# VectorE's side work dealt out slot by slot, and one head of a search copied by ScalarE

## The chip, the cores and the metric

One core of one Trainium2 chip runs the whole program. The metric is device microseconds of one execution, as the median over several runs. TensorE (PE, with its weight loads PEld), VectorE (DVE), ScalarE (ACT), GpSimd (POOL) and SyncE (SP, which only issues DMAs here) run side by side and wait for each other by semaphores.

## The reference

One transformer block with modulation from a condition `c`, in fp32: 4 sequences of 2048 tokens, 256 channels, 8 heads of 32; then a mixture of experts with 2 shared and 16 routed experts of width 128, 4 of them for each token.

```
mod = (silu(c) @ wmod) -> sa, ca, ga, sb, cb, gb
ga, gb = sign * max(|.|, 0.25)
h = layernorm(x) * (1 + ca) + sa
x = x + ga * attn(h)        # causal softmax(q k / sqrt(32) + head_scale * geo(q, k)) @ v, then @ w_out
h = layernorm(x) * (1 + cb) + sb
x = x + gb * ffn(h)
ffn(h): shared = sum over 2 experts of gelu(h @ up) @ down
        probs = softmax(h @ router); gate = the 4 largest probs, else 0
        routed = sum over 16 experts of (gelu(h @ up) * gate) @ down
```

## The kernel before

**Tiling.** The tokens are 16 blocks of 512 rows (`QB`), four to a sequence; block i has place qb = i mod 4 in its sequence and sees qb + 1 blocks of keys. The 8 heads are two groups (g = 0, 1) of four, whose 32 rows each lie in the four row groups of TensorE.

**Searches.** Softmax needs each row's maximum first. `max_steps` makes one search step for 128 queries, 512 keys and four heads: `scores(t, ch)` computes the scores into two PSUM places (`ps`, each of two heads, 128x1024), and VectorE adds the causal mask where the step lies on the diagonal and reduces each place to its maxima (`parts`). When a group's steps are done, `split` and `turn` carry the maxima to TensorE as three bf16 pieces (`mT`). Block i + 1's steps run while block i is worked on.

**Sums.** `sum_steps(i, g, oT)` has one slot for each 128 keys: `probabilities(kb)` multiplies scores of four heads into two PSUM places (`st`), takes the maxima off in the same accumulation, and ScalarE's exps write `p`; `weigh(kb, 0)` and `weigh(kb, 1)` add to the numerators (`av`) and denominators (`dv`). After a group's last slot `finish` (line 735) copies both out of PSUM (ScalarE `num`, VectorE `rd`), and VectorE takes one reciprocal and one product of 128x512 into `oT`. A block has ks = 8, 16, 24 or 32 slots, half of them for each group.

**PSUM.** Three places of two banks go round (`pair`, tag m) for `ps`, `st` and small products during the sums; two single banks (`accp`) hold `av` and `dv`, and in the stretches between the sums every small product (`single`).

**Order.** It is written out by hand, and every engine keeps its program order (`Pinned`). For each block there are two stretches:

- *Between the sums* (`fill_in`): projections of a coming block, the router's logits and the shared experts of block i - 2, tiles of the routed experts, the output product of block i - 1, and as many search steps as that work covers.
- *The sums*: `part` is a list of (place, step), sorted by place. Slot n's scores stand at n, its weighted sums at n + 1.3 and n + 1.6, the searches that are left (`rest`) at n + 0.5, and ticks at n + 0.9. The side work of VectorE is strung along by `when`, from assumed durations: the first norm of coming blocks, the router's choice for block i - 2 (`choice_steps`), at a group's end its places (`place_steps`), and the second norm of block i - 1.

**Experts.** Routed tokens are handled in five groups of 2, 3, 3, 3 and 3 blocks; the last two blocks go through all experts densely. For a group `place_steps` finds each token's row in a buffer sorted by expert, and GpSimd scatters the rows there, 16 indirect DMAs and one load for each block (`scatters`). When the last is issued `tiles_of` starts the group's expert tiles (`px`, `pu`, `py`), whose rows and weights SyncE fetches. The results are gathered by GpSimd and added up by VectorE (`combine`, result `sum`). `tick` issues one scatter or gather, and lets a combine run two ticks after its last gather.

**Names in the profile.** The recording helper gives all lines as L52 (L72 for the scatters), so groups are told apart by tile names: `pk` and `pc` are the products that count tokens of an expert, `selb` and `seen` their inputs, `rank` the copy of `pk`; `xnb` the second norm's rows, `ptb` their transposes; `rsb` the norm's power.

Of the kernel before, what the change touches and what calls it, by code (L numbers as in the profile page):

```python
# [19 lines left out]
P = 128  # L20
# [72 lines left out]
def adaln_block_kernel(  # L93
# [324 lines left out]
    def max_steps(i, g):  # L418
# [6 lines left out]
        def scores(t, ch):  # L425
# [15 lines left out]
            for a, both in enumerate(halves):  # L441
                if ch == qb:
                    edge = both[:, :, w - P : w]
                    nc.vector.tensor_tensor(edge, edge, c_pair, ALU.add)
                nc.vector.tensor_reduce(
                    parts[:, t, 2 * a : 2 * a + 2, ch], both[:, :, :w], AX.X, ALU.max
                )
# [51 lines left out]
    def tick(add=True):  # L499
        for due in sums_due:  # L500
            due[0] -= 1
        if add and sums_due and sums_due[0][0] <= 0:
            sums_due.pop(0)[1]()
        if scatters:
            scatters.pop(0)()
            return
        if not gathers and ready and len(sums_due) < 2:
            gathers.extend(ready[0][0])
        if gathers:
            gathers.pop(0)()  # L510
            if not gathers:
                sums_due.append([2, ready.pop(0)[1]])
# [150 lines left out]
    def sum_steps(i, g, oT):  # L663
# [5 lines left out]
        pts = {}  # L669
# [46 lines left out]
        def weigh(kb, s):  # L716
# [15 lines left out]
            if s and kb == nkb - 1:  # L732
                finish()

        def finish():
            rd = once.tile([P, QB], F32, tag="rd", name=f"rd{i}_{g}")
            num = once.tile([P, QB], F32, tag="num", name=f"num{i}_{g}")
            nc.scalar.copy(num, sums[0])
            nc.vector.tensor_copy(rd, sums[1])
            nc.vector.reciprocal(rd, rd)  # L740
            nc.vector.tensor_tensor(oT[:, g, :], num, rd, ALU.mult)

        return [
# [6 lines left out]
        ]  # L750

# [68 lines left out]
    def turn_steps(i):  # L820
# [14 lines left out]
        def logits():  # L835
# [10 lines left out]
            logs[i] = small.tile([P, TT, R], F32, tag="log", name=f"log{i}")  # L846
# [4 lines left out]
    def choice_steps(i, group):  # L851
# [18 lines left out]
        def choose():  # L870
# [7 lines left out]
            top = small.tile([P, TT, 8], F32, bufs=1, tag="rtop", name=f"rtop{i}")  # L878
            rest = small.tile([P, TT, R + 8 - TOPK], F32, bufs=1, tag="rrest", name=f"rrest{i}")
            for t in range(TT):  # L880
                nc.vector.max(top[:, t, :], pr[:, t, :])
                nc.vector.match_replace(rest[:, t, :], top[:, t, :], pr[:, t, :], -1.0)
            sel = small.tile([P, TT, R], F32, bufs=1, tag="sel", name=f"sel{i}")
            nc.vector.tensor_scalar(sel, rest[:, :, :R], 0.0, None, ALU.is_lt)
# [11 lines left out]

        def count():

            sel = held["sel"]
# [4 lines left out]
        def earlier_ones():  # L904
            selb = held["selb"]
            t0 = group.blocks.index(i) * TT
# [8 lines left out]
            nc.vector.tensor_copy(group.rank[:, t0 : t0 + TT], pk)  # L915
            for t in range(TT):
                nc.vector.tensor_tensor(group.seen, group.seen, selb[:, t, :], ALU.add)

        def weights():

            pr, sel = held["pr"], held["sel"]
            t0 = group.blocks.index(i) * TT
            met = small.tile([P, TT, R], F32, bufs=1, tag="met", name=f"met{i}")
            flat = sel.rearrange("p t e -> p (t e)")
# [3 lines left out]
            hot = group.hot[:, t0 : t0 + TT]  # L928
            shape = [P, TT, TOPK, R]
            nc.vector.tensor_tensor(  # L930
                hot,
# [4 lines left out]
            nc.vector.tensor_tensor(hot, hot, sel.unsqueeze(2).broadcast_to(shape), ALU.mult)  # L936
            wide = once.tile(shape, F32, tag="hotp", name=f"hotp{i}")
            nc.vector.tensor_tensor(
                wide, hot, pr[:, :, :R].unsqueeze(2).broadcast_to(shape), ALU.mult
# [17 lines left out]
        steps = [differences, exponentials, choose]  # L957
        if group is not None:
            return steps + [count, weights, earlier_ones]
        return steps + [across]  # L960

    def place_steps(group):

        n, tok = group.n, group.tok
        held = {}

        def tiles_of_experts():
            pc = single([P, R], f"pc{n}")
            nc.tensor.matmul(pc, lhsT=unit3, rhs=group.seen, start=True, stop=True)
            ci = small.tile([P, R], I32, bufs=1, tag="ci", name=f"ci{n}")  # L970
            nc.vector.tensor_scalar(ci, pc, float(P - 1), None, ALU.add)
# [10 lines left out]
        def owners():  # L982
            shape = [P, MAXT, R]
            past = once.tile(shape, BF16, tag="num", name=f"past{n}")
            nc.vector.tensor_tensor(
                past,
                tile_no.unsqueeze(2).broadcast_to(shape),
# [3 lines left out]
            who = small.tile([P, MAXT], F32, bufs=1, tag="who", name=f"who{n}")  # L991
            nc.vector.tensor_reduce(who, past, AX.X, ALU.add)
            nc.vector.tensor_scalar(group.owner, who, float(R - 1), None, ALU.min)

        def places():
            shape = [P, tok, R]
            rank, hot = group.rank[:, :tok], group.hot[:, :tok]
            nc.vector.tensor_tensor(
                rank, rank, held["first"].unsqueeze(1).broadcast_to(shape), ALU.add
            )  # L1000
            shape = [P, tok, TOPK, R]
            nc.vector.tensor_tensor(hot, hot, rank.unsqueeze(2).broadcast_to(shape), ALU.mult)
            at = small.tile([P, 3 * TT, TOPK], F32, bufs=1, tag="atf", name=f"atf{n}")
# [538 lines left out]
```

## Time and profile before

| what | us |
|---|---|
| median of 5 runs (2571.86 to 2588.51) | 2586.14 |
| the profiled execution | 2581.32 |
| its span, first to last instruction | 2579.6 |
| the sixteen sums together | 1262.1 |
| the stretches between, before and after | 1317.5 |
| of these, from the last sums to the end | 273.2 |
| mean granted TensorE clock | 0.95 |

The costliest groups of VectorE and ScalarE in the profiled execution:

| group | count | mean ns | busy us |
|---|---|---|---|
| VectorE maxima, 128x1024 | 448 | 1221 | 530.1 |
| VectorE maxima, narrower | 192 | 426 to 959 | 133.0 |
| VectorE mask on the diagonal, 128x256 | 256 | 427 | 109.3 |
| VectorE reciprocal of the denominators, 128x512 | 32 | 3353 | 107.3 |
| ScalarE exps, 128x1024 | 448 | 1021 | 434.2 |

How to read it: the span is one execution on the chip. An engine's busy time is a mean over stretches with different limits, so the share of VectorE (55%) does not say where it is late. The granted clock tells in which time TensorE ran at half speed. A wait is put down to what came last.

### The profile page before, as it was taken

To read this page: it belongs to the slowest core of one execution; us is meant where nothing else is said; L and a number is where in the kernel's file an instruction comes from. 1 tells how busy PE (TensorE), PEld (TensorE's weight loads), DVE (VectorE), ACT (ScalarE), POOL (GpSimd) and SP (SyncE) were. 2 spreads that over 40 slices of the span, in tenths; PEclk is the share of its full clock that TensorE was granted. 3 is DMA by queue.
4 is the path that set the end of the run, shared out by engine and by line. 5 is a ranking of instruction groups with operands and counts; after the bars stand their busy time and mean duration, and the time that the engine had idled before them with its cause. 6 is when DMAs were issued, how large, how long until landed. Compare 5 with 4: busy or idle time off the path is not lost.

```text
span 2579.6 us, 42345 instructions
## 1 busy us (share of the span) xinstructions
PE 2412.5 (94%) x16961; PEld 1171.5 (45%) x16961; DVE 1406.6 (55%) x2609; ACT 978.7 (38%) x1372; POOL 702.0 (27%) x740
## 2 busy tenths in 40 slices
PE   7999999999999899999999999999898999998987
PEld 4433423345544223355654335254544643335754
DVE  5576655526676845247564666346664564422235
ACT  2223233543343234544343334543343345453320
POOL 3201010411133134202014422401442025544324
PEclk9889899999999899999999999998999999998999
DMA  2300401434432112223641225233636843236943
GB/s 86 117 1 9 147 9 59 139 123 147 157 120 64 39 54 81 74 74 102 228 133 66 82 96 180 74 104 99 206 128 210 260 146 95 89 135 234 329 151 110
DMA packets 219701, 306.90 MB, mean 119 GB/s; under 512 B 18544, under 2 KB 158832, under 8 KB 219504
## 3 DMA queue, kind: packets, MB, share of 16 engines
q1 hardware_dynamic: 192720, 228.89, 26.8%
q0 software_dynamic: 25536, 73.43, 8.9%
q8 instruction: 134, 2.20, 0.3%
q10 hardware_dynamic: 1248, 1.86, 0.2%
q14 instruction: 63, 0.52, 0.1%
HBM read 193.49 MB, written 114.82 MB: 120 GB/s over the span
## 4 chain that ended last, share of the span: by engine, by line
PE 77%; DVE 10%; ACT 4%; issue 4%; POOL 2%; DMA 2%; another core or an unknown queue 0%; SPq 0%; POOLq 0%; ACTq 0%; DVEq 0%
PE st L52 15%; PE ps L52 12%; PE av L52 10%; PE dv L52 8%; PE pu L52 7%; PE py L52 5%; DVE parts L52 4%; PE po L52 3%; PE ppq L52 2%; PE px L52 2%; PE pv L52 2%; PE ppk L52 2%; PE pd_s L52 1%; PE pd L52 1%; ACT p L52 1%
## 5 line engine op out<-in xcount | busy, mean ns | idle before, releaser
L52 DVE TENSOR_REDUCE parts<-ps 128x2 f32<-128x1024 f32 (+3 forms) x640 | 662.6, 1062 | 357.9 <-PE ps L52 336.4
L52 ACT ACTIVATE p<-st 128x1024 f32<-128x1024 f32 (+3 forms) x640 | 538.8, 893 | 677.9 <-PE st L52 628.8
L52 PE MATMUL st<-qT,kv 32*128 32x512 f32 (+3 forms) x2560 | 428.4, 597 | 33.5 <-DVE parts L52 18.6
L52 PE MATMUL ps<-kv,qT 32*128 32x512 f32 (+3 forms) x2560 | 390.5, 610 | 19.3 <-DVE parts L52 10.1
L52 POOL DMA_INDIRECT got<-yg,at x224 | 220.1, 983 | 396.0 <-ACT p L52 128.2
L52 PE MATMUL av<-p,kv 128*32 128x512 f32 (+3 forms) x2560 | 318.7, 566 | 6.7 <-issue 3.0
L52 PE MATMUL dv<-p,ones 128*32 128x512 f32 (+3 forms) x2560 | 311.5, 553 | 1.3 <-issue 1.1
L72 POOL DMA_INDIRECT xg<-rows,at x219 | 213.2, 973 | 292.5 <-ACT p L52 133.6
L52 PEld LDWEIGHTS st<-qT,kv 32*128 32x128 f32 x2560 | 143.9, 191 | 302.9 <-issue 211.1
L52 DVE TENSOR_TENSOR ps<-ps,cmask 128x256 f32<-128x256 f32 x256 | 109.3, 427 | 264.0 <-PE ps L52 234.6
L52 PEld LDWEIGHTS ps<-kv,qT 32*128 32x128 f32 x2560 | 128.6, 192 | 211.6 <-issue 110.6
L52 POOL TENSOR_TENSOR x<-x,tmps 128x512 f32<-128x512 f32 x28 | 35.4, 1263 | 621.4 <-DVE tmps L52 621.4
L52 PE MATMUL py<-wt,tact 128*128 128x256 f32 x608 | 162.2, 400 | 7.3 <-ACT xt L52 3.5
L52 PE MATMUL st<-mT,unit 3*128 3x512 bf16 (+3 forms) x1280 | 165.9, 355 | 0.0
L52 PEld LDWEIGHTS pu<-xt,wt 128*128 128x128 f32 x1216 | 149.0, 195 | 28.9 <-issue 10.2
L52 PE MATMUL pu<-xt,wt 128*128 128x128 f32 x1216 | 157.3, 282 | 2.7 <-ACT y L52 0.7
L52 PEld LDWEIGHTS dv<-p,ones 128*32 128x32 f32 x2560 | 76.6, 113 | 179.4 <-issue 171.8
L52 DVE SCALAR_TENSOR_TENSOR sum<-got,weight,sum 128x256 f32<-128x256 f32 x168 | 83.1, 494 | 121.2 <-DMA got<-yg,at 116.5
L52 ACT COPY y<-py 128x512 f32<-128x512 f32 x152 | 89.0, 586 | 152.0 <-PE py L52 148.0
L52 PEld LDWEIGHTS py<-wt,tact 128*128 128x128 f32 x608 | 108.8, 193 | 55.8 <-issue 13.2
L52 ACT COPY xt<-px 128x512 f32<-128x512 f32 x152 | 86.9, 586 | 99.3 <-PE px L52 95.1
L52 PEld LDWEIGHTS av<-p,kv 128*32 128x32 f32 x2560 | 54.1, 110 | 147.8 <-issue 124.0
(287 smaller groups left out, 2433.0 us busy)
## 6 DMA issues: line engine op xcount, KB each, us to landing
wt<-experts SPq DMA_DIRECT2D x304, 256.0 KB
xr<-xg SPq DMA_DIRECT2D x76, 512.0 KB
yg<-y SPq DMA_DIRECT2D x76, 512.0 KB
xg<-zeros SPq DMA_DIRECT2D x16, 1024.0 KB
xin<-in_x SPq DMA_DIRECT2D x16, 512.0 KB
x<-in_x SPq DMA_DIRECT2D x16, 512.0 KB
h2d<-xnb POOLq DMA_DIRECT2D x14, 512.0 KB
pre<-x POOLq DMA_DIRECT2D x14, 512.0 KB
```

Of the source, the lines that this page charges most:

```text
L52: made = call(*args, **kwargs)
L72: made = call()
```

## The change

1. During the sums a search step splits its first place. ScalarE copies the second head to SBUF (`second`, two buffers), VectorE reduces the first head in PSUM, then the whole second place, then the copy. Between the sums nothing changes.
2. `finish` is taken apart. The copies `num` and `rd` follow their group's last slot; reciprocal and product are four steps of 128 columns (`divide`). The first group's go into the slots after the middle of the sums, the second group's between the first pieces of the next stretch.
3. The router's choice, the places, and `combine` are cut into smaller steps. `pk` and the count `pc` are copied out by ScalarE; they and the steps that need another engine's result wait a slot. The scatters of each block are released after that block's places, before the owners of the tiles are found.
4. In the sums each step gets a price, and `put` gives it the first slot with room: 2.2 us, or 1.4 where there is a search; what finds no room goes into the last slot.
5. A combine starts three ticks after its last gather, and its second half a tick later.
6. At the end of the program the last block's second norm moves behind the start of the last group's tiles, and the first product of the dense experts behind the first step of the choice.

The diff, cut to its core:

```diff
@@ scores
+            def top(scores, h0, h1, mask):
                 if ch == qb:
-                    edge = both[:, :, w - P : w]
-                    nc.vector.tensor_tensor(edge, edge, c_pair, ALU.add)
-                nc.vector.tensor_reduce(
-                    parts[:, t, 2 * a : 2 * a + 2, ch], both[:, :, :w], AX.X, ALU.max
-                )
+                    edge = scores[..., w - P : w]
+                    nc.vector.tensor_tensor(edge, edge, mask, ALU.add)
+                nc.vector.tensor_reduce(parts[:, t, h0:h1, ch], scores[..., :w], AX.X, ALU.max)
+
+            if state["summing"]:
+                copy = probs.tile([P, QB], F32, bufs=2, tag="second", name=f"second{i}_{g}_{t}_{ch}")
+                nc.scalar.copy(copy[:, :w], halves[0][:, 1, :w])
+                top(halves[0][:, 0, :], 0, 1, cmask)
+                top(halves[1], 2, 4, c_pair)
+                top(copy, 1, 2, cmask)
+            else:
+                top(halves[0], 0, 2, c_pair)
+                top(halves[1], 2, 4, c_pair)
@@ tick
-            sums_due.pop(0)[1]()
+            sums_due[0][1].pop(0)()
+            if not sums_due[0][1]:
+                sums_due.pop(0)
...
-                sums_due.append([2, ready.pop(0)[1]])
+                sums_due.append([3, ready.pop(0)[1]])
@@ sum_steps
-        def finish():
-            rd = once.tile([P, QB], F32, tag="rd", name=f"rd{i}_{g}")
-            num = once.tile([P, QB], F32, tag="num", name=f"num{i}_{g}")
-            nc.scalar.copy(num, sums[0])
-            nc.vector.tensor_copy(rd, sums[1])
-            nc.vector.reciprocal(rd, rd)
-            nc.vector.tensor_tensor(oT[:, g, :], num, rd, ALU.mult)
+            if kb == nkb - 1 and s:
+                held["rd"] = once.tile([P, QB], F32, tag="rd", name=f"rd{i}_{g}")
+                nc.vector.tensor_copy(held["rd"], sums[1])
+            elif kb == nkb - 1:
+                held["num"] = once.tile([P, QB], F32, tag="num", name=f"num{i}_{g}")
+                nc.scalar.copy(held["num"], sums[0])
+
+        def divide(t):
+            own = slice(t * P, (t + 1) * P)
+            rd = held["rd"]
+            nc.vector.reciprocal(rd[:, own], rd[:, own])
+            nc.vector.tensor_tensor(oT[:, g, own], held["num"][:, own], rd[:, own], ALU.mult)
@@ choice_steps
-            nc.vector.tensor_copy(group.rank[:, t0 : t0 + TT], pk)
+            nc.scalar.copy(group.rank[:, t0 : t0 + TT], pk)
...
+        steps = [
+            (0.6, 0, differences),
+            (0.0, 1, exponentials),
+            (0.6, 1, shares),
+            (0.9, 0, lambda: choose(0)),
+            (0.9, 0, lambda: choose(1)),
+            (0.4, 0, chosen),
+        ]
+        if group is None:
+            return [s for _, _, s in steps] + [across]
+        return steps + [
+            (0.0, 1, earlier_ones),
+            (0.7, 0, seen),
+            (0.7, 0, met),
+            (0.4, 0, picked),
+            (0.9, 0, weights),
+        ]
@@ place_steps
-        return [tiles_of_experts, owners, places], sends
+        per_block = 1 + TT * TOPK
+        steps = [(0.0, 1, counted), (1.2, 1, tiles_of_experts)]
+        for j in range(len(group.blocks)):
+            now = sends[j * per_block : (j + 1) * per_block]
+            steps += [(1.3, 0, lambda j=j: places(j)), (0.0, 0, lambda now=now: scatters.extend(now))]
+        return steps + [(1.4, 0, lambda: past(0)), (1.4, 0, lambda: past(1)), (0.2, 0, owners)]
@@ between the sums
+            for n, s in enumerate(ends):
+                (lead or mid).insert(2 * n + 1, (0.001, s))
@@ the sums
+        searched = {int(0.93 * (n + 0.5) / len(rest) * ks) for n in range(len(rest))}
+        room = [1.4 if n in searched else 2.2 for n in range(ks)]
+
+        def put(steps, lo, hi):
+            at, shift = int(lo), (hi - lo) / max(1, len(steps))
+            for n, (us, wait, step) in enumerate(steps):
+                at = min(max(at + wait, int(lo + n * shift)), ks - 1)
+                while room[at] < us and at < ks - 1:
+                    at += 1
+                room[at] -= us
+                part.append((at + 0.6, step))
+            return at
+
+        def norm(steps):
+            us = [0.6] * TT + [0.2] + [0.4] * TT + [0.0] * TT
+            return [(u, 1 if n == TT + 1 else 0, s) for n, (u, s) in enumerate(zip(us, steps))]
+
+        put([(1.2, 0, s) for s in divided], ks // NQ + 1, ks // NQ + 1)
         if qb == 0:
-            steps += [(1.0, s) for j in fresh[:1] for s in first_norm_steps(j)]
+            for j in fresh[:1]:
+                put(norm(first_norm_steps(j)), 1, 1)
...
-            steps += list(zip((1.0, 1.0, 3.5, 0.5, 2.5, 2.0), choice_steps(i - 2, group)))
+            steps = choice_steps(i - 2, group)
             if i - 2 == group.blocks[-1]:
-                place, sends = place_steps(group)
-                steps += list(zip((2.0, 3.0, 4.0), place)) + [(0.0, lambda: scatters.extend(sends))]
+                steps += place_steps(group)
                 filled = group
+            put(steps, 1, 1)
         if i:
-            steps += [(1.0, s) for s in second_norm_steps(i - 1)]
+            steps = norm(second_norm_steps(i - 1))
...
+            put(steps, 1, 0.85 * ks)
...
-        at, scale = 0.0, min(1.0, 0.95 * length / max(sum(us for us, _ in steps), 1.0))
-        for us, s in steps:
-            part.append((when(1.0 + scale * at), s))
-            at += us
@@ the end of the program
-    begin += choice[2:3] + downs[:1] + choice[3:] + downs[1:] + free(second_norm_steps(j))
+    begin += choice[2:-1] + downs[:1] + choice[-1:] + downs[1:]
...
-    late = turn_steps(j) + choice + more
+    norms = second_norm_steps(j)
+    late = turn_steps(j) + choice[:1] + more + choice[1:]
```

## The prediction

> **What bounds the kernel now.** I read the page's head first: who is busy, which clock TensorE was granted, and by whom the last chain of work runs.
>
> ```profile
> span 2579.6 us, 42345 instructions
> PE 2412.5 (94%) x16961; PEld 1171.5 (45%) x16961; DVE 1406.6 (55%) x2609; ACT 978.7 (38%) x1372; POOL 702.0 (27%) x740
> ...
> PEclk9889899999999899999999999998999999998999
> ...
> PE 77%; DVE 10%; ACT 4%; issue 4%; POOL 2%; DMA 2%; another core or an unknown queue 0%; SPq 0%; POOLq 0%; ACTq 0%; DVEq 0%
> ```
>
> TensorE sets the end, VectorE is only half busy, and yet VectorE holds 10% of the chain. So VectorE is late at places, not overloaded. To see where, I cut the span into the sixteen blocks' sums (scores, exps, weighted sums) and the stretches between them, and asked for busy times by window. Columns: length, then busy time of PE, PEld, DVE, ACT and POOL with instruction counts, then granted clock, DMA share, GB/s. Blocks 2 and 6 and the sum over all sixteen sums:
>
> ```profile
> 302.80:420.80 118.00, 113.08 (x893) 35.40 (x893) 68.27 (x114) 44.09 (x53) 8.88 (x11) 0.94 0.14 47
> 849.40:981.70 132.30, 120.96 (x894) 36.05 (x894) 81.27 (x144) 44.11 (x53) 38.75 (x42) 0.91 0.14 46
> sum 1262.10, PE 1201.39 PEld 388.86 DVE 663.53 ACT 578.42 POOL 403.19; mean PE 75.09 PEld 24.30 DVE 41.47 ACT 36.15 POOL 25.20
> ```
>
> The same TensorE work takes 14 us longer in block 6, with 13 us more on VectorE. In the sums TensorE idles 1262.1 - 1201.4 = 61 us; and (1 - clock) x length, summed over the sixteen rows, is 68 us of lost clock. So 129 us is the most that the sums can give back. Which waits they are, the view of TensorE's waits says (total, times, longest):
>
> ```profile
> PE st L52 <- DVE parts L52: 18.6, 21, 2.3
> ...
> PE st L52 <- ACT p L52: 10.0, 13, 1.6
> PE ps L52 <- ACT p L52: 9.1, 7, 1.8
> ...
> PE pc L52 <- DVE seen L52: 4.9, 3, 2.3
> PE pk L52 <- DVE selb L52: 4.3, 2, 2.5
> ...
> PE st L52 <- DVE rank L52: 4.1, 4, 1.4
> PE px L52 <- DVE rd L52: 3.8, 1, 3.8
> ```
>
> The ACT lines are mostly the first exps of a block; the change doesn't touch them. The DVE lines are its target. One of them in the timeline (start, duration, instruction, idle before it), and in the view by windows the stretch that follows, with its clock:
>
> ```profile
> 929.17 3.35 DVE L52 RECIPROCAL rd<-rd 128x512 f32<-128x512 f32 x1
> ...
> 934.54 1.23 PE L52 MATMUL st<-qT,kv 32*128 32x512 f32 x2 [1.99 <-DVE parts L52]
> ```
>
> ```profile
> 934.30:941.10 6.80, 6.56 (x28) 1.64 (x32) 1.26 (x4) 1.94 (x2) 0.96 (x1) 0.50 0.06 22
> ```
>
> A reciprocal of 3.35 us makes the search behind it late, TensorE stands 1.99 us for a PSUM buffer, and then runs 6.8 us at half clock: 3.4 us more. Last, two slots (one key block each), without a search and with one:
>
> ```profile
> 1022.48 1.14 PE L52 MATMUL st<-qT,kv 32*128 32x512 f32 x8
> ...
> 1023.45 0.40 PE L52 MATMUL st<-mT,unit 3*128 3x512 bf16 x4
> ...
> 945.69 2.36 DVE L52 TENSOR_REDUCE parts<-ps 128x2 f32<-128x1024 f32 x2 [2.37 <-PE ps L52]
> ...
> 946.63 1.47 PE L52 MATMUL st<-qT,kv 32*128 32x512 f32 x8
> ...
> 948.22 1.94 ACT L52 ACTIVATE p<-st 128x1024 f32<-128x1024 f32 x2 [2.79 <-PE st L52]
> ```
>
> The same eight st records take 1.14 us and 1.47 us. The second pair of heads takes the buffer that the search's first place held, and VectorE leaves that one 945.69 + 1.18 = 946.87, after the st's start at 946.63. That is 0.33 us per searched slot.
>
> **The change part by part.** Durations are from the profiled execution; its own time is 2581.3 us, 4.8 below the median of 2586.1, so a gain is taken off the first and carried to the second.
>
> *Reciprocal in four pieces.* In blocks 0, 2, 6 and 10 the middle reciprocal ends in a wait of about 2.0 us: 4 x 2.0 = 8. The half clock behind it is 3.4 us above; I take 3 each: 12. **-20.** A quarter costs, between the rows of 512 columns (3.353) and of 4 (0.178), 0.95 us; a product of 128 columns, between 0.204 at 16 and 0.707 at 512, 0.32. Four of each are 5.1 us for 4.1: 32 x 1.0 = 32 us more on VectorE, hidden in its 1173 idle us as long as each quarter stays within its slot; 32 is its price otherwise. The last group's four now stand between the next stretch's first pieces, before the output product that needs them.
>
> *The router's chain, dealt out.* pk, pc and rank waits are 4.3 + 4.9 + 4.1 = 13.3; of the 18.6 on parts, 8 are the reciprocals', and half of the rest, 5.3, I give to this chain (the copies to ScalarE, and the search that queues behind it). Nine waits in seven stretches of clock at 3 us are 21. Together 40. But blocks 4, 8 and 12 have eight slots only: worked through by hand, the new placing loads their last slot with 6.9, 6.9 and 15.0 us by its own prices, where two rank waits (1.24 each), pk and pc (1.78 + 2.32) and some 8.5 us of clock sit now. I count those 15 as not gained: **-25**; bounds 0 and 40. A late copy of the denominators (rd, one wait of 1.77 and its clock) is met half the time: **-3**.
>
> *The copy.* No row shows ScalarE copying while VectorE reduces. The nearest: a 128x512 copy from PSUM took ScalarE 0.59, a reduce of 512 elements VectorE 0.69 and of 1024 1.22; a reduce of 768 took 0.95 from SBUF and 0.96 from PSUM. So the first place is free 0.69 us after its matmuls for 1.18 now, at 946.4, before the st wants it. 808 ps records lie in the sums, 8 a search: 101 searches. All 0.33 us: 33. Where the search is narrow its reduce is short and nothing is to be had; 448 of 640 reduces are full width: **-24**; bounds 0 (ScalarE's exps end at 950.16, the matmuls at about 950.4, so little room) and 33. VectorE pays 0.69 + 1.22 + 0.69 = 2.60 for 2.44, and on the diagonal one more mask of about 0.3 us: under 25 us in all, in slots of 4.7 us. On ScalarE 101 x 0.59 = 60 us stand between the exps; what queues behind a copy is the next slot's exps, which wait for later matmuls anyway, and the scatters that are tied to ScalarE's last instruction.
>
> *The tail.* Eight GpSimd modulates (6.1 us) and a power (1.0) move from in front of the last four scatters to behind them. The first scatter of that block comes one to two slots later than now, some three scatters of 1.26 us. 7.1 - 3.8 = 3.3 us earlier for the expert rows, for which TensorE waits 7.29 us, and half of 3.4 us of clock: **-5**, bounds 0 and 11. The router's second wait there (6.4 us) keeps its chain. SyncE's fetch of those rows moves with the last scatter.
>
> *What is late next.* In blocks 4 and 8 the last slot holds two quarters, the router's end and the second norm. The norm's first scaled row comes about 4 us later than now (two quarters with products 2.5, plus what waited for pk), and the 6.1 us of GpSimd behind it end that much later; TensorE's transposes of that row tile follow within 0.2 us of their end now. So 4 us and 3.4 of clock, twice: 15; block 12, which already waits 3.8 us for rd, 2 more: **+17**; bounds 0 and 82 (below). Combines of 2.7 us (0.37 + 3 x 0.49 + 0.45 + 0.43), now in two parts, aren't in the plan of any slot: **+5**.
>
> Sum: -20 - 25 - 3 - 24 - 5 + 17 + 5 = -55. **2581.3 - 55 = 2526 for a profiled execution, 2531 for the median.**
>
> A rule that speaks against a third of this. The Trainium skill, "TensorE: Matmul & The Clock Gate", section "Part 1: The HAM clock gate (the "warmup" mystery)", has the clock halved after at least one idle window of about 3.4 us. The row above has it halved after 1.99 us of idling. By the rule no wait of 2.5 us or less would cost clock, the clock terms (12 + 12.5 + 1.7 + 1.7 - 6.8 = 21) would fall out, and the median would be 2552; I go by the row.
>
> **The rivals.** *The copy brings nothing.* ScalarE comes to it late, or VectorE's longer search (+0.16 us x 101 = 16) is felt. For it: only 0.3 us between the exps' end and the matmuls'. Against it: VectorE has 2.4 us idle in front of each search. 2531 + 24 + 16 = 2571.
>
> *The ends of the short blocks set the time (slower).* Place: the last slots of blocks 0, 4, 8, 9 and 12, planned at 2.4, 6.9, 6.9, 4.3 and 15.0 us: 35.5 on VectorE, and in three of them 7.1 us of GpSimd behind the norm: 21. The denominators' copy is queued behind all of it, and TensorE's next stretch needs that PSUM buffer. If all is waited out with 5 us of clock each: 82 for 17, and the router's 25 is not gained: 2531 + 65 + 25 = 2621. For it: block 12 does this now, rd 5.5 us after its sums. Against it: VectorE works ahead of TensorE in unsearched slots. It decides from 72 us, 14 an end.
>
> *More than forecast.* The ends cost nothing, the copy and the router give all they hold, and the sums run at full clock: 2531 - 17 - 9 - 15 - 10 = 2480.
>
> **How the numbers follow.** About 0.5%, 13 us, can be told from no change here. Forecast (2505 to 2560): 0.47. More than forecast: 0.16. Copy without effect: 0.21, half of it inside 13 us of 2586. Short ends: 0.16, all slower. So faster 0.73, within 0.5% 0.11, slower 0.16. The range takes the upper rivals in until under two tenths are left out: 2480 to 2605; the time is the forecast's, 2531.
>
> **What would show it.** Step 1: four reciprocals of about 0.95 us per group, and no st wait of 2 us behind them in blocks 0, 2, 6, 10. Step 2: the pc, pk and rank waits gone from TensorE's list in blocks 2, 6, 10, 11, 14; block 6's sums near block 10's length. Step 3: st records in searched slots at 1.14 us, slots at 4.4 instead of 4.7. Tail: the last scatter some 3 us sooner after the sums. Ends: px or ptb waits of 4 to 10 us just behind the sums of blocks 4, 8 and 12. I am wrong if the granted clock stays at 0.95 with the waits gone; if searched slots stay at 4.7 us; or if the first group's 34 loads and scatters, for which I count 35 issues in block 3, miss its end, so that expert tiles fall one stretch later.

## The result, and the profile after

| | us |
|---|---|
| changed kernel, median of 29 runs (2580.09 to 2599.89) | 2590.2 |
| kernel before beside it, median of 55 runs | 2583.2 |
| ratio, 95% interval | 1.0029 (1.0019 to 1.0038) |
| forecast | 2531 (2480 to 2605) |

The change makes the kernel 7 us slower, where 55 us less were forecast. The page of its profile, head and clock:

```profile
span 2584.0 us, 42896 instructions
...
PE 2416.7 (94%) x16961; PEld 1181.0 (46%) x16961; DVE 1441.5 (56%) x2997; ACT 1044.4 (40%) x1511; POOL 700.2 (27%) x740
...
PEclk9889799999999899999999999998998999999999
```

Busy times and the clock look much as before; ScalarE has 66 us more work. The stages have changed. The view by windows, the sums of blocks 2 and 6 and then all sixteen sums (length, busy PE, PEld, DVE, ACT, POOL, granted clock, DMA share, GB/s):

```profile
308.90:425.50 116.60, 114.20 (x893) 35.41 (x893) 69.82 (x146) 55.51 (x75) 8.95 (x11) 0.95 0.14 48
...
863.90:980.20 116.30, 113.44 (x894) 35.16 (x894) 84.23 (x186) 55.72 (x76) 28.65 (x31) 0.97 0.11 36
...
sum 1230.00, PE 1199.27 PEld 390.63 DVE 700.74 ACT 644.86 POOL 388.95; mean PE 74.95 PEld 24.41 DVE 43.80 ACT 40.30 POOL 24.31
```

Block 6 came from 132.3 to 116.3 us and is now as long as blocks 2 and 10 (116.6 and 116.3), as forecast. All sums are 32 us shorter, although 21 searches more lie in them (block 14's, below); without block 14 they are 70 us shorter. The same view of the fifteen stretches between the sums ends in

```profile
sum 979.00, PE 902.45 PEld 580.15 DVE 575.75 ACT 304.10 POOL 161.72; mean PE 60.16 PEld 38.68 DVE 38.38 ACT 20.27 POOL 10.78
```

against 940.7 us before: 38 us longer. So the gain in the sums is real, and the stretches gave it back. TensorE's waits (total us, times, longest):

```profile
PE px L52 <- DMA xr<-xg: 13.8, 2, 9.9
...
PE ptb L52 <- POOL xnb L52: 8.8, 7, 3.3
...
PE st L52 <- DVE parts L52: 7.8, 17, 1.4
PE pu L52 <- DMA wt<-experts: 7.8, 12, 2.1
...
PE pta L52 <- ACT num L52: 5.2, 4, 3.8
```

The waits that the change aimed at went: st for VectorE's maxima from 18.6 to 7.8, pc from 4.9 to 1.4, pk and rank gone. What came instead stands in the stretches: ptb for the second norm's rows (1.2 us before), pta for the numerators' copy (1.7 before; `pta` are the transposes of the first norm's rows, which take a bank that this copy leaves), and pu for the experts' weights (0.5 before).

Last the copy. A searched slot of block 2 in the timeline (start, duration, instruction, idle before it):

```profile
373.33 1.82 PE L52 MATMUL ps<-kv,qT 32*128 32x512 f32 x8
...
375.24 0.62 ACT L52 COPY second<-ps 128x512 f32<-128x512 f32 x1
375.44 1.90 PE L52 MATMUL st<-qT,kv 32*128 32x512 f32 x6
375.89 1.82 DVE L52 TENSOR_REDUCE parts<-ps 128x1 f32<-128x512 f32 x2 [2.20 <-ACT second L52]
```

VectorE was idle for 2.20 us and starts at 375.89, after ScalarE's copy has ended at 375.86, though it reads the other head, in another bank. The copy does not run beside the search; it stands in front of it. The groups say the same of all full-width searches (busy us, mean ns, idle before and its releaser):

```profile
L52 DVE TENSOR_REDUCE parts<-ps 128x1 f32<-128x512 f32 x93 | 64.2, 690 | 141.5 <-ACT second L52 140.8
...
L52 ACT COPY second<-ps 128x512 f32<-128x512 f32 x93 | 54.7, 588 | 43.2 <-PE ps L52 20.7 <-ACT p L52 18.5 <-issue 3.3
```

The first place comes free after 0.59 + 0.69 = 1.28 us, where one reduce of 1.22 did it before. Slots of the sums whose keys are off the diagonal, with one search and no other work of TensorE in them, have a median of 4.85 us for 4.74.

### The profile page after: what moved, and what is told of

It reads as the page before. It is cut to its first block, busy times and chain, and to the rows that moved or that the text cites. A ratio compares the mean times of both kernels' runs of the same rounds, so it can differ in the third digit from the quotient of the medians.

```text
span 2584.0 us, 42896 instructions
## 1 busy us (share of the span) xinstructions
PE 2416.7 (94%) x16961; PEld 1181.0 (46%) x16961; DVE 1441.5 (56%) x2997; ACT 1044.4 (40%) x1511; POOL 700.2 (27%) x740
## 5 line engine op out<-in xcount | busy, mean ns | idle before, releaser
L52 DVE TENSOR_REDUCE parts<-ps 128x2 f32<-128x1024 f32 (+6 forms) x640 | 604.4, 972 | 337.3 <-PE ps L52 187.3
L52 PE MATMUL ps<-kv,qT 32*128 32x512 f32 (+3 forms) x2560 | 401.9, 618 | 22.0 <-DVE parts L52 11.9
L52 PE MATMUL av<-p,kv 128*32 128x512 f32 (+3 forms) x2560 | 308.3, 552 | 3.4 <-DVE rd L52 1.9
L52 PE MATMUL dv<-p,ones 128*32 128x512 f32 (+3 forms) x2560 | 300.8, 539 | 0.0
L52 PEld LDWEIGHTS st<-qT,kv 32*128 32x128 f32 x2560 | 144.1, 186 | 282.6 <-issue 132.3
L52 DVE TENSOR_TENSOR ps<-ps,cmask 128x256 f32<-128x256 f32 (+1 forms) x256 | 103.4, 404 | 264.5 <-ACT second L52 158.5
L52 PEld LDWEIGHTS ps<-kv,qT 32*128 32x128 f32 x2560 | 135.5, 194 | 230.5 <-issue 85.5
L52 DVE RECIPROCAL rd<-rd 128x128 f32<-128x128 f32 x128 | 120.8, 943 | 0.7
L52 POOL TENSOR_TENSOR x<-x,tmp 128x512 f32<-128x512 f32 x32 | 40.6, 1270 | 277.9 <-DVE tmp L52 237.6
```

What stands on the lines that cost most here:

```text
L52: made = call(*args, **kwargs)
```

## The experiments

The runs fell on five chips, and the kernel before itself took 2556 us on two of them and 2583 to 2587 on the others, so kernels are compared by their ratio to the kernel before on the same chip, and side by side on one chip where that is possible.

**1. The copy.** Four kernels on one chip (before: 2556 us). *spread*: the change without the copy.

```diff
-            if state["summing"]:
-                copy = probs.tile(...)
...
+            top(halves[0], 0, 2, c_pair)
+            top(halves[1], 2, 4, c_pair)
```

> The changed kernel without the copy: in the sums too, VectorE reduces both search places with two heads each; all the rest of the change stays. Theory A (the copy never runs beside VectorE: VectorE's first reduce waits until ScalarE's copy has ended, so the first place comes free after 0.59 + 0.69 = 1.28 us instead of 1.22): the copy is a small loss in each of the 120 searched slots, about 0.1 us, so about 2590 - 10 = 2580 us (2572 to 2588), and full searched slots near 4.75 us instead of 4.85. Rival B (the copy carries its share of what the sums gained, and the stretches between gave it back): 10 to 24 us slower, 2600 to 2614, the sums of blocks 6 and 10 longer by 2 to 5 us each.

*apart*: the change, with the order between the copy and the first reduce taken out where the search only reads.

```diff
+            def alone(made):
+                if ch < qb:
+                    own = f"heads{i}_{g}_{t}_{ch}"
+                    tc.declare_no_dep(made.ins, group=own, reason="a bank of its own")
+                    tc.add_to_no_dep_group(own, made.ins)
...
-                nc.scalar.copy(copy[:, :w], halves[0][:, 1, :w])
-                top(halves[0][:, 0, :], 0, 1, cmask)
+                alone(nc.scalar.copy(copy[:, :w], halves[0][:, 1, :w]))
+                alone(top(halves[0][:, 0, :], 0, 1, cmask))
```

> The changed kernel, with the order between ScalarE's copy and VectorE's first reduce taken out of the program where the search is not on the diagonal (76 of the 120 searches in the sums); the two heads lie in different banks and both are only read there. Theory A (it is the program that makes VectorE wait): the reduce of the first head starts with the copy, the first place comes free after 0.69 us, off-diagonal searched slots go to 4.4 to 4.5 us; 76 x 0.35 = 27 us less, about 2563 us (2550 to 2580). Rival C (the two engines are slowed by each other at PSUM, or something else than this place sets the slot): reduces of 0.69 us grow to 1.0 or more, or the slots stay at 4.8 us; 2585 to 2595.

*copy_only* and *copy_apart*: the kernel before with the copy alone, with the wait and without it (both with two buffers for the router's logits instead of three, to make room).

> The kernel before with the copy alone (and two buffers for the router's logits instead of three, to make room). Theory A: with the wait in it the copy costs some 0.1 us in each of 101 searched slots, and VectorE ends a search 0.7 us later: 5 to 15 us slower than before, 2588 to 2600. The forecast's term: 24 us faster, 2560.

> The kernel before with the copy alone, and the order between the copy and the first reduce taken out off the diagonal (some 60 of 101 searches). Theory A: 60 x 0.35 = 21 us faster than before less 4 for the diagonal ones, about 2567 (2555 to 2580), so some 25 us below the same kernel with the wait. Rival C: no faster than before, 2583 to 2600.

| kernel | median us | ratio (95%) |
|---|---|---|
| spread | 2553.3 | 0.9991 (0.9976 to 1.0006) |
| apart | 2545.0 | 0.9960 (0.9945 to 0.9976) |
| copy_only | 2577.9 | 1.0088 (1.0069 to 1.0107) |
| copy_apart | 2558.8 | 1.0008 (0.9997 to 1.0019) |

By these ratios *spread* is 10 us faster than the changed kernel (0.9991 against 1.0029), as theory A had it. With the wait the copy alone costs 22 us, more than the 5 to 15 expected; taking the wait out gives 19 of them back, but the kernel is then no faster than before, as rival C had it. The wait came from the program: the framework orders the two readers of one PSUM tile. In *apart*, a slot with copy and reduce side by side, and behind the dots the slot that answers to the one above:

```profile
359.42 1.82 DVE L52 TENSOR_REDUCE parts<-ps 128x1 f32<-128x512 f32 x2 [0.96 <-PE ps L52]
359.46 0.59 ACT L52 COPY second<-ps 128x512 f32<-128x512 f32 x1 [1.05 <-PE ps L52]
...
363.05 1.93 DVE L52 TENSOR_REDUCE parts<-ps 128x1 f32<-128x512 f32 x2 [0.89 <-PE ps L52]
...
363.99 1.17 PE L52 MATMUL st<-qT,kv 32*128 32x512 f32 x6
```

VectorE no longer waits for the copy, and six st records take 1.17 us for 1.90. Of the 76 full-width searches off the diagonal, 60 have copy and first reduce side by side; in the others, as in the second slot, ScalarE comes to its copy later. Yet the true overlap is worth only 8 us over no copy at all (2553.3 to 2545.0), and in the kernel before nothing. The median of those slots goes from 4.73 (*spread*) to 4.57, not to 4.4: 0.16 us a slot where the forecast had 0.33. What is left may be ScalarE's own work: eight ps records take 1.81 us at 361.89 in this profile (1.18 at 342.59), since their second place is one that the slot's exps, 1.94 us from 361.50, have still to leave. I read this from the order of the places; it was not tried alone.

**2. The stretches.** Four kernels on one chip (before: 2583 us), all from the changed kernel. *zero*: `insert(2 * n + 1, (0.0, s))` for `(0.001, s)`.

> The changed kernel, with the second group's divides priced at 0.0 instead of 0.001 between the first pieces of the next stretch. Theory D (the 0.004 of four such prices turns an exact tie in the planner, 65.45 against 65.75 - 0.3, so that one search fewer is placed among the work of the stretches before blocks 4, 5, 8 and 13 and three searches come back to back at their ends): those stretches come back by about 3, 2, 5 and 2 us; 12 us less than the changed kernel, so about 5 us below the kernel before. Rival E (these stretches lose only by the late denominators and by the clock): no change, 7 us above the kernel before.

*tiles*: the last scatters are issued at a block's end.

```diff
         run(part)
+        while scatters and len(scatters) < 3:
+            scatters.pop(0)()
         state["summing"] = False
```

> The changed kernel, with one or two scatters that are left at the end of a block's sums issued there, so that the expert tiles of blocks 11 to 13 are free for the stretch before block 14, as in the kernel before. Theory F (that stretch lost its cover: one scatter of 51 was left, the tiles came a stretch later, and 21 searches moved into block 14's sums): the stretch before block 14, its sums and the stretch behind them together go from 266 us back to 239 to 245; some 20 us less than the changed kernel, 13 us below the kernel before (range -20 to -5). Rival G (the same work only lies elsewhere, and TensorE is as busy): no change beyond 5 us.

*late*: steps without room go behind the denominators' copy; the pieces stay where they are.

```diff
-        def put(steps, lo, hi):
+        def put(steps, lo, hi, late=1.65):
...
-                part.append((at + 0.6, step))
+                part.append((at + (0.6 if room[at] >= 0 else late), step))
...
-        put([(1.2, 0, s) for s in divided], ks // NQ + 1, ks // NQ + 1)
+        put([(1.2, 0, s) for s in divided], ks // NQ + 1, ks // NQ + 1, 0.6)
```

> The changed kernel, with the steps that find no room placed behind the copy of the second group's denominators instead of in front of it; the divides stay where they are. Theory H (the copy rd that is late by 2 to 13 us at the end of blocks 0, 1, 4, 5, 8, 9, 12 and 14 keeps a PSUM bank, and the next stretch goes to and fro on the other one): the stretches before blocks 5, 6, 9 and 13 get 3 to 6 us shorter each; 10 us less than the changed kernel (0 to 20). Rival I (what is moved behind, the second norm above all, makes its own readers late): waits of the transposes ptb for xnb grow by as much; 0 to 10 us more than the changed kernel.

*all_apart*: all of it, with *apart* and a second buffer for `num`.

> All of it together on the changed kernel: the copy beside the first reduce off the diagonal (one buffer for it), the price of 0.0, the last scatters issued at a block's end, the steps without room behind the denominators' copy, and a second buffer for the numerators. If the terms add (18 for the copy, 12 for the prices, 20 for the tiles, 10 for the ends, 5 for the numerators in the stretch before block 1): 7 - 65 = 58 us below the kernel before, ratio about 0.978, which is what the forecast had for the change as it stands. If the stretches give back again what the sums gain: ratio 0.99 or more.

| kernel | median us | ratio (95%) |
|---|---|---|
| zero | 2589.9 | 1.0026 (1.0004 to 1.0047) |
| tiles | 2557.6 | 0.9894 (0.9864 to 0.9923) |
| late | 2597.4 | 1.0065 (1.0042 to 1.0088) |
| all_apart | 2558.0 | 0.9902 (0.9873 to 0.9931) |

*tiles* is the largest single finding: one scatter, of the 51 issues of blocks 11 to 13, was left when the sums of block 13 ended, and so the expert tiles of that group started one stretch later. The three windows around block 14 (stretch, sums, stretch) in the changed kernel:

```profile
1947.30:1983.60 36.30, 33.79 (x156) 18.33 (x156) 31.50 (x38) 4.14 (x7) 15.24 (x15) 0.81 0.47 159
1983.60:2107.40 123.80, 118.25 (x893) 35.62 (x893) 91.40 (x197) 55.43 (x75) 40.24 (x43) 0.94 0.19 56
2107.40:2213.00 105.60, 93.96 (x580) 80.75 (x578) 15.56 (x32) 48.21 (x87) 9.88 (x9) 0.98 0.88 296
```

and in *tiles*:

```profile
1949.40:2093.10 143.70, 130.22 (x836) 88.93 (x836) 85.84 (x104) 49.71 (x87) 16.38 (x16) 0.95 0.75 246
2093.10:2170.80 77.70, 75.40 (x723) 24.35 (x722) 41.89 (x111) 44.77 (x55) 40.97 (x44) 0.99 0.36 109
2170.80:2185.00 14.20, 13.40 (x67) 10.18 (x67) 7.47 (x12) 4.17 (x7) 5.73 (x6) 1.00 0.10 29
```

Together 265.7 against 235.6 us. The work is the same, but its place isn't: 21 searches that lay among the expert tiles now lie in block 14's sums. There a search costs (123.8 - 77.7) / 21 = 2.2 us; in the stretches it costs (143.7 + 14.2 - 36.3 - 105.6) / 21 = 0.8. In the last stretch VectorE then has 15.6 us of work in 105.6, and TensorE waits for the experts' weights (pu).

*zero* did what was worked out and gave no time. The planner asks whether its place has reached `free - 0.3`; worked out from the prices in the code, before block 8 that is 65.45 against 65.45, and four prices of 0.001 let the rounding fall to the other side. With 0.0 the stretches before blocks 4, 5, 8 and 13 came back by 3.9, 1.8, 3.5 and 3.9 us. But the one before block 12 sits on such a tie too, which had gone the better way, and lost 4.9, and the sums of blocks 5, 7 and 13 lost 7.9, two of them with one search more in them.

*late* went as rival I had it. TensorE's wait for the norm's rows in that profile, 8.8 us in the changed kernel:

```profile
PE ptb L52 <- POOL xnb L52: 22.0, 12, 8.5
```

What stood in front of the copy was itself waited for. In *all_apart* the steps moved behind left four scatters at block 13's end, so its condition of fewer than three did not issue them and the tiles came late again: its three windows are 280 us long. It doesn't tell whether the terms add.

**3. The parts by themselves**, on one chip (before: 2587 us), all with the last scatters issued. *whole_tiles*: no copy, reciprocals whole as before; what remains is the side work dealt out by slots, the cut combines and the tail.

> The changed kernel without its copy and without its divided reciprocals (one reciprocal and one product of 512 columns at a group's end, as before), and with the last two scatters of blocks 11 to 13 issued at the end of block 13's sums. What is left of the change is the side work dealt out by slots, the cut combines and the tail. Forecast's terms for these: -25 - 5 + 5 and most of the ends' +17: 10 to 25 us below the kernel before, ratio 0.990 to 0.996. If the dealing out is worth nothing alone: ratio 1.0.

*spread_tiles*: the pieces added. *apart_tiles*: the truly parallel copy added. *best*: that, with two buffers for `num` and the price 0.0 except before block 12.

> The same with the reciprocals and products in four pieces as in the change; still no copy. The forecast's term for the pieces (20 us less in the sums of blocks 0, 2, 6 and 10, 5 each, and nothing in the stretches): ratio 0.008 below that of the kernel with whole reciprocals. Theory J (the pieces also cost where they now stand: the ties of the four prices in the stretches before blocks 4, 5, 8 and 13, 13 us as measured, and the second group's divides behind the first transposes there): the sums gain 20, the stretches lose 10 to 20, ratio the same within 0.004.

> The changed kernel with the copy truly beside the first reduce off the diagonal, and with the last scatters issued at block 13's end. If what these two gave alone adds (0.7% and 1.35%): ratio 0.982. Against the kernel without a copy and the same scatters: 0.003 lower, as between the two without the scatters, which is 8 us for the copy where the forecast had 24.

> The changed kernel with the copy beside the first reduce (one buffer), the last scatters issued at block 13's end, a second buffer for the numerators, and the second group's divides priced at 0.0 except in the stretch before block 12, where the tie goes the other way. If the terms add: the prices 13 us less in the stretches before blocks 4, 5, 8 and 13 (some 5 given back in the sums), the numerators 2.5: ratio 0.977 to 0.980, some 55 us below the kernel before, near the forecast's figure for the change as it stands. If the prices are again given back elsewhere: 0.982.

| kernel | median us | ratio (95%) |
|---|---|---|
| whole_tiles | 2533.9 | 0.9791 (0.9761 to 0.9822) |
| spread_tiles | 2537.2 | 0.9817 (0.9784 to 0.9850) |
| apart_tiles | 2540.1 | 0.9813 (0.9783 to 0.9844) |
| best | 2523.3 | 0.9755 (0.9724 to 0.9786) |

The dealing out, with the cut combines and the tail, is worth 53 us here (42 when it ran again, below). The pieces and the copy bring nothing that stands clear of the noise. Why the pieces are worth nothing stands in the two sums of windows, sixteen sums and fifteen stretches, of *whole_tiles*:

```profile
sum 1210.10, PE 1165.01 PEld 381.61 DVE 657.87 ACT 581.63 POOL 398.62; mean PE 72.81 PEld 23.85 DVE 41.12 ACT 36.35 POOL 24.91
...
sum 950.50, PE 895.52 PEld 569.40 DVE 589.04 ACT 305.00 POOL 155.23; mean PE 59.70 PEld 37.96 DVE 39.27 ACT 20.33 POOL 10.35
```

and of *spread_tiles*:

```profile
sum 1170.50, PE 1141.52 PEld 377.17 DVE 650.70 ACT 581.53 POOL 392.71; mean PE 71.34 PEld 23.57 DVE 40.67 ACT 36.35 POOL 24.54
...
sum 985.50, PE 914.91 PEld 578.65 DVE 615.63 ACT 306.15 POOL 157.94; mean PE 60.99 PEld 38.58 DVE 41.04 ACT 20.41 POOL 10.53
```

39.6 us less in the sums, 35.0 more in the stretches. TensorE's waits in *whole_tiles*:

```profile
PE st L52 <- DVE parts L52: 17.9, 17, 3.2
...
PE ptb L52 <- POOL xnb L52: 2.0, 2, 1.0
PE pta L52 <- ACT num L52: 1.9, 4, 0.5
```

and in *spread_tiles*:

```profile
PE pta L52 <- ACT num L52: 8.8, 6, 3.8
PE ptb L52 <- POOL xnb L52: 7.7, 6, 2.4
...
PE st L52 <- DVE parts L52: 3.7, 7, 1.0
```

In the sums the waits for VectorE's maxima go. In the stretches TensorE's idling grows from 55 to 71 us and its lost clock, (1 - clock) x length over the rows, from 37 to 58. Of the idling, the numerators' copy (3.8 us of it behind block 0) and the second norm's rows behind blocks 4, 8 and 12 make up 12.6 us more. The wait for the denominators' copy (pta for rd) does not grow: 5.0 us in *whole_tiles*, 0.9 in *spread_tiles*.

*best* is 17 us faster than *apart_tiles* on the same chip. Its stretches are 19 us shorter (977.5 for 996.8), and pta waits 1.4 us for the numerators instead of 7.1. So with the expert tiles in time the second buffer and the prices together do count; which of the two, was not tried alone.

**4. Which pieces cost the stretches**, on one chip (before: 2557 us). Without the copy: only the first group's reciprocal in pieces, only the second's, the first with two buffers for `num`, and that with the parallel copy.

```diff
                 nc.vector.tensor_copy(held["rd"], sums[1])
+                if g:
+                    nc.vector.reciprocal(held["rd"], held["rd"])
+                    nc.vector.tensor_tensor(oT[:, g, :], held["num"], held["rd"], ALU.mult)
...
-        return steps, [lambda t=t: divide(t) for t in range(TT)]
+        return steps, [] if g else [lambda t=t: divide(t) for t in range(TT)]
```

> No copy, last scatters issued at block 13's end, and of the reciprocals only the first group's in pieces; the second group's is whole again at the end of the sums. Theory K (the stretches lose by the second group's pieces standing among their first steps): it keeps most of the 39 us gain of the sums and gives back most of the 38 us loss of the stretches; ratio 0.966 to 0.972 against 0.979 with both whole and 0.982 with both in pieces. Theory L (the stretches lose because the first group's pieces fill the last slots and make the denominators' copy late): ratio 0.979 to 0.983.

> The other half: the first group's reciprocal whole after the middle of the sums, the second group's in pieces in the next stretch. Theory K: the sums gain little (the whole reciprocal in the middle makes a search late), the stretches lose; ratio 0.985 to 0.992, the slowest of the four. Theory L: the last slots are free, the stretches as with whole ones; ratio 0.976 to 0.980.

> As with the first group's pieces alone, with a second buffer for the numerators: ScalarE's copy of the second group no longer waits for the first group's last product. If that wait is what is left in the stretches behind the short blocks: 3 to 8 us less than without it; if TensorE's bank was held by the denominators' copy anyway: the same within 2 us.

> As the one before, with the copy beside the first reduce off the diagonal (one buffer). If VectorE's reduces in the sums still hold TensorE: 5 to 10 us less than without a copy (off-diagonal slots 4.57 us for 4.73). If the copy only moves the lateness to the ends of the blocks, as it did beside the kernel with all pieces: the same within 4 us.

| kernel | median us | ratio (95%) |
|---|---|---|
| first_pieces | 2508.8 | 0.9814 (0.9793 to 0.9836) |
| second_pieces | 2532.1 | 0.9895 (0.9874 to 0.9915) |
| first_num | 2506.8 | 0.9800 (0.9780 to 0.9821) |
| first_apart | 2510.8 | 0.9819 (0.9798 to 0.9839) |

Since chips differ, *whole_tiles* and *first_num* ran once more side by side (before: 2585 us):

> The kernel with whole reciprocals, no copy, and the last scatters issued at block 13's end, for the comparison on one chip. On a chip where the kernel before takes 2556 us: ratio 0.985 to 0.990; where it takes 2585: 0.979.

> The first group's reciprocal in pieces, the second's whole, two buffers for the numerators, for the comparison on one chip. By the idle time of TensorE in the profiles (45 + 55 us in sums and stretches with whole ones, 23 + 67 with these) 10 us of idling are saved, and some 8 to 20 of clock behind it: ratio 0.005 to 0.011 below that of the whole ones. If the stretches give back all: the same within 0.002.

2542.8 us, 0.9830 (0.9805 to 0.9855), and 2524.9 us, 0.9761 (0.9733 to 0.9788). So the first group's pieces, with the second buffer, bring 18 us net: the sums are 37.0 us shorter (1170.4 for 1207.4), the stretches 19.1 longer (976.3 for 957.2). Beside them the second group's pieces bring a loss, as far as ratios from different chips tell it (0.9817 with both kinds, 0.9761 with the first's). Both kinds make the stretches longer (950.5 us with none and 985.5 with both on one chip, 969.8 with the second's and 975.7 with the first's on another). Neither K nor L is the whole story. Beside the first group's pieces alone, the second buffer for `num` and the parallel copy are each within 4 us of nothing, though the buffer takes pta's longest wait for the numerators from 3.8 to 0.5 us. *first_again* and *best* are the fastest, 2.4% below the kernel before, each against the kernel before on its own chip; they weren't run side by side.

## Why the prediction was wrong

Along a chain of kernels on chips where the kernel before takes 2583 to 2587 us, the change falls apart like this (whole_tiles, spread_tiles, tiles, changed kernel):

| step | ratio after it | worth, us | forecast, us |
|---|---|---|---|
| side work dealt out, combines, tail | 0.9791 (again: 0.9830) | -54 (-44) | -25 - 3 + 5 - 5, and most of +17 |
| reciprocals in pieces | 0.9817 | +7 | -20 |
| the copy | 0.9894 | +20 | -24 |
| expert tiles one stretch late | 1.0029 | +35 | 0 |

The sum is 8 us where 55 less were forecast. The last two steps compare kernels that did not run side by side and are uncertain by some 8 us each: the changed kernel against *spread*, both with the tiles late, puts the copy at 10 us, and the tiles then at 45.

*The router's chain, dealt out*: right in kind, too small. In *whole_tiles* the sums of block 6 are 11 us shorter, those of blocks 11 and 14 8 each (13, 8 and 7 when it ran again). Blocks 9 and 15, which I had not named, are 5 and 9 us shorter, but they are 5 and 8 shorter in *copy_only* too, whose side work lies as before, so this can't be put down to the dealing out. Not counting blocks 4, 8 and 12 was right: their sums are 2.0, 2.0 and 4.2 us shorter, and the stretches behind them 3.2, 4.6 and 2.4 longer. The waits for pc and rank are gone; pk, with the reciprocals whole, still waits 5.7 us.

*Reciprocal in four pieces*: the quarter was sized right (943 ns, forecast 950), and the sums gained 40, not 20: the waits for VectorE's maxima fell by 14 us with the pieces, where I gave them 8. The step that failed is "The last group's four now stand between the next stretch's first pieces", priced at nothing, and so is that the first group's four, in the last slots, make late what follows them. The stretches lost 35, most visibly by the numerators' copy and the second norm's rows; 20 of the 35 lie before blocks 4, 5, 8 and 13, where *zero* gave 13 back, so the ties of the four prices are part of it. How the 35 divide among these causes stays open.

*The copy*: the step that failed is "the first place is free 0.69 us after its matmuls". Its premise, that the engines run side by side, was written in the change and not in the program, and it fell: 1.28 us. The rival "The copy brings nothing", at 2571, was nearest to the time, by luck: it took a late ScalarE or VectorE's longer search for the cause, and none of the other misses was in it. With the premise made true the sums gain 4 to 7 us, not 24, near the lower of my two bounds; its reason, little room between the exps' end and the matmuls', fits the profile but was not tried alone.

*What is late next*: +17 (0 to 82) was the right place and too small a size. Against the kernel before, the stretches of *tiles* are 56 us longer, the 35 above among them; by windows (996.4 - 920.0) - (940.7 - 892.4) = 28 us of it are idling of TensorE, and the lost clock, (1 - clock) x length summed over the rows, grew by 31. The ends of short blocks were the rival on the slower side, and the sum had them for blocks 4, 8 and 12 alone; the wait for the numerators behind block 0 (3.8 us) was in none of the terms. The ptb waits behind blocks 4, 8 and 12, for which I had 4 to 10 us each, are 1.0, 1.5 and 6.4 us in the changed kernel.

*Expert tiles one stretch late*: named as a thing that would make me wrong, for the first group's 34 issues. That group made it. The last, blocks 11 to 13 with 51 issues, missed by one. The forecast put this term at nothing. I counted the issues of one group and not of the others.

*Tail*: -5 forecast, not shown. The stretch behind the last sums is 1.9 us shorter, but in *copy_only* and *copy_apart*, whose tail is as before, it is 2.4 and 3.1 shorter, and the wait for the expert rows grew from 7.29 to 9.9 us.

*The clock*: the forecast held a rule of the Trainium skill against the row of 1.99 us ("TensorE: Matmul & The Clock Gate", "Part 1: The HAM clock gate (the "warmup" mystery)": an idle window of about 3.4 us). The runs side with the row: in the changed kernel the sums of block 14 have no wait of TensorE over 1.8 us, and a clock of 0.94. From the kernel before to the changed one TensorE's idling in the sums fell from 61 to 31 us and its lost clock from 67 to 30; in the stretches idling rose from 48 to 77 and lost clock from 31 to 62. So the lost clock went with the idling in both directions, as the forecast had priced it.

## What to carry to other kernels

Work that is placed on two engines "side by side" needs a look at the waits in the program: two readers of one tile can be ordered although nothing in the data asks for it. In a schedule that runs by counts and thresholds, a small move can miss a threshold by one, and then a whole stage shifts; count every group that must end in time, and treat exact ties as open. What is taken out of a loaded stage has to be followed into the next one: gains of 40 us in the sums were paid back as 35 in the stretches behind them.

## What the runs showed of the hardware

- ScalarE and VectorE read the two banks of one PSUM tile at the same time without slowing each other: the reduce of 512 elements took 690 ns with the wait (changed kernel) and without it (*apart*, 60 of 93 side by side with their copy), the copy 588 ns in both (93 each).
- The same program differs by 1.2% between chips: the median of the kernel before was 2557 us on one (granted clock 0.952 to 0.958 in its runs) and 2587 on another (0.946 to 0.958).
